# A fused two-layer graph kernel on one core: five edits at the seam between its layers and around its walk

## The chip, the core and the metric

The program runs on one core of a Trainium2 chip. Its engines are TensorE (PE; its weight loads are listed apart as PEld), VectorE (DVE), ScalarE (ACT), GpSimd (POOL) and SyncE (SP), which here issues nearly all DMAs. Each engine works through its own list of instructions, and semaphores tie them together. The metric is the time of one execution on the device in microseconds; the comparison uses the median of several runs.

## What is computed

There are 2708 nodes with 256 features, and an adjacency matrix `adj` (2708 x 2708, float32). Everything is computed in float32. Cut to what matters:

```python
# layer 0
R = adj + I;  R = R / R.sum(-1)
for n in range(2):
    A  = top_p(softmax(q(Xa) @ k(Xa).T), 0.9)   # rows renormalised
    Xf = R @ Xf                                 # the "walk"
    Xa = A @ Xa                                 # the "attention"
    Z += Xf @ U1[n].T + Xa @ U2[n].T
h = layernorm(x + Z) * ln_g + ln_b
x = layernorm(x + h)
# layer 1: graph attention, 4 heads of 64
Wh = x @ W;  e_ij = leaky_relu(s_i + s_j), masked where adj is zero (diagonal kept)
x = layernorm(x + softmax_j(e) @ Wh)
```

## The kernel before

**Tiles.** The 2708 rows are cut into 22 tiles: 16 of 128 rows and 6 of 110. The last three tiles are called late (`LATE = 3`).

**Layer 0** is `fast_layer0`. It has two steps `s`, 0 and 1. In each step the attention of tile `t` runs on TensorE in six groups of up to four source tiles (`weigh`, L274: transposes of the kept probabilities, L266, copies of them by ScalarE, L271, and matmuls, L284). Beside it runs the walk, which multiplies by the adjacency matrix; it is put together from products of mixed blocks (the "mixes", written to DRAM during step 0), seven products for each of 11 pairs of row tiles, and is the generator `walks` (L1034). The walk of step 0 starts when step 0's attention is over, and reaches into step 1; the walk of step 1 ends close to the end of step 1's attention.

**Slots.** The order of work on TensorE, VectorE, ScalarE and GpSimd is written out by hand: after each group of the attention, `slot` (L1292) advances several generators by one `yield`:

- `going`: searches for the probabilities to keep of a coming tile (`search`, L971). Its first part is `scores` (L780): logits by matmul (L791) in three pieces, each exponentiated by ScalarE (L795). The first two pieces come in the slot in which the search begins, the third one slot later. A search of tile `t + 3` begins at the fifth group of tile `t`.
- `doing`: what remains to be done for a row tile after its walk or attention: `after_walk0`, `after_attention0`, `finish`, and the early loads of layer 1's masks (`early_bar`).
- `mixing` and `stream`: the mixes, and so many matmuls of the walk (L1109) as the slot's allowance says.

`finish(t, ...)` (L1261) closes a tile in step 1. ScalarE scales the walk's rows `xw` by `rinv`, the inverse row sums (L1265). GpSimd adds up x and the terms of step 0 and 1: `ca` (x), `cb` (a stored term), `xw`, and the attention's rows `held[t]` (L1270 to L1272), and adds the bias to `ca` (L1273). For tiles that aren't late, two layer norms follow (`norms`, L186) and then `sources` (L159), which projects the row by layer 1's weights: transposes (L165), a copy (L167), a matmul (L171) and seven small readings by ScalarE (L175 to L181). The late tiles wait until the walk is over (`walked`), since their sums are written over the walk's operand `xe`, and get their norms in layer 1 (`prepared`, L1665).

**Banks.** Once the walk has begun, the logits and the projections of `sources` take turns in the same pool of two PSUM buffers (`ps_lg`, through `free_bank`, L650).

**Rows of step 0.** `after_walk0` (L1194) scales and adds on GpSimd, yields once, and stores the rows to DRAM (L1200). They are read back when the walk of step 0 ends.

**SyncE** is not among the engines whose order is fixed by hand: where each of its DMAs stands in its list is set by a planner, which places a DMA once its buffer is free and its sources are there, by its own estimates of time. The list is then executed in order.

**Layer 1** (`layer1`) goes over three groups of target tiles (8, 8 and 6); for each, over all 22 source tiles `j`. VectorE makes the weights `pt` of four heads from the targets, the source's `tj` and the mask (L1606); TensorE adds up values (L1618) and denominators (L1628), two source tiles at a time. The mask is loaded (L245) and made 0 or 1 by ScalarE (L247, L248). The targets of the first group are two tiles from the pool `ep` (three buffers, shared with the probabilities of layer 0): `share` (L208) turns the sources' terms and stores them, `spread` (L219) broadcasts them back to all partitions, two DMAs for each of the two tiles. In step 1, `share(0, ...)` stands at the start of tile 20 and `spread(0, ...)` at that of tile 21 (L1315 to L1319).

**Memory.** Pools of layer 1 take the memory that pools of layer 0 leave. Among the latter is `keep`, which holds the walk's and the attention's operands and, by L632, `rinv`:

```python
rinv = keep.tile([P, NT], F32, name="rinv")
```

Tiles of the pool `const` stay for the whole program.

Of the kernel before, what the change touches and what calls it, by code (L numbers as in the profile page):

```python
# [45 lines left out]
def kernel(  # L46
# [169 lines left out]
        nc.scalar.activation(line[:k, :m], tr[:k, 0, :m], AF.Exp, scale=1.0 - NEG_SLOPE)  # L216
        nc.sync.dma_start(shared[g], line[:k, :m])

    def spread(g, r):  # L219

        lines = shared[g].rearrange("(t h) m -> h t m", h=H)
        n = len(spans[g]) * rows[spans[g][0]]
        for k in range(2):
            for h in range(2):
                nc.sync.dma_start(
                    r[k][:, h, :n].rearrange("p (t m) -> p t m", t=len(spans[g])),
                    lines[2 * k + h].partition_broadcast(P),
                )
# [22 lines left out]
            nc.vector.tensor_tensor(own, own, ident[:k, :k], op=ALU.max)  # L251
        yield bar

    def room(pool):

        return [
            pool.tile([P, N], F32, name="e")[:, : 2 * GW].rearrange("p (h i) -> p h i", h=2)
            for _ in range(2)
        ]

    def turned(e, m, n, pool, ps, copy):
# [290 lines left out]
    def fast_layer0(ep, adjp):  # L552
# [76 lines left out]


        kT = [wk.tile([P, HN], F32, name="junk"), keep.tile([P, HN], F32, name="kT1")]
        rinv = keep.tile([P, NT], F32, name="rinv")  # L632

        BLOCKS = ("D11", "S2", "S3", "S1", "D22", "S4")
        mixed = {
# [398 lines left out]
        def walks():  # L1034
# [19 lines left out]
            def beside(s, t):  # L1054

                m = rows[t]
                if s and t >= NT - LATE:
                    ca = x_late[:, t - NT + LATE, :]
                    nc.gpsimd.memset(ca[:, 0:1], 0.0)
                else:  # L1060
                    ca = finp.tile([P, D], F32, name="ca", bufs=4)
                if not s:
                    nc.sync.dma_start(ca[:m], c1[t][:m])
                    return ca, None
                cb = finp.tile([P, D], F32, name="cb")
                nc.sync.dma_start(ca[:m], x[off[t] : off[t + 1], :])
                nc.sync.dma_start(cb[:m], c2[t][:m])
                if t in c3:
                    assert t in stored
                    held[t] = finp.tile([P, D], F32, name="cc")  # L1070
                    nc.sync.dma_start(held[t][:m], c3[t][:m])
                return ca, cb
# [6 lines left out]
            for at, (s, i, n) in enumerate(queue):  # L1079
# [17 lines left out]
                        home = dict(X=k, Y=1 - k, Z=k, W=1 - k)  # L1097
                if at % 7 == (3 if s else 0):
                    aside = {t: beside(s, t) for t in (a, b)}
                start = chain not in use  # L1100
                if start:
                    pool, label = (ps_wk, f"walk{home[chain]}") if home[chain] < 2 else (ps_at, "att")
# [91 lines left out]
        def after_walk0(t, xw, ca, _):  # L1194
            m = rows[t]
            yield
            nc.gpsimd.tensor_scalar(xw, xw, rinv[:m, t : t + 1], None, op0=ALU.mult)
            nc.gpsimd.tensor_add(xw, xw, ca[:m])
            yield
            nc.sync.dma_start(xmd[:m, t], xw)  # L1200
            rows_kept.append(t)

# [44 lines left out]
        def terms2(t, xT):  # L1247
# [10 lines left out]
            nc.scalar.copy(ba[:m, t, :], cy[:m, D : 2 * D])  # L1258
            nc.sync.dma_start(c2[t][:m], cs[:m])

        def finish(t, xw, ca, cb):  # L1261

            m = rows[t]
            yield
            nc.scalar.activation(xw, xw, AF.Copy, scale=rinv[:m, t : t + 1])  # L1265
            while t not in held or (t >= NT - LATE and not walked):
                yield
            late = t >= NT - LATE
            xt = xe[:m, t, 0:D] if late else lines[t % len(lines)][:m]
            nc.gpsimd.tensor_add(xt, ca[:m], cb[:m])  # L1270
            nc.gpsimd.tensor_add(xt, xt, xw)
            nc.gpsimd.tensor_add(xt, xt, held.pop(t)[:m])  # L1272
            nc.gpsimd.tensor_add(ca[:m], ca[:m], b_sb[:m])  # L1273
            if not late:
                yield
                yield from norms(t, xt, ca)
                yield from sources(t, rowp, free_bank, src=xt)
                nc.sync.dma_start(xd[:m, t], xt)


        going, doing, stored, owing = [], [], set(), set()
        early, walked, blending, begun, rows_kept = [], [], [], [], []
        ready, held = {}, {}
        stream, mixing = walks(), mixes()
# [2 lines left out]
        def advance(parts):  # L1287
            for g in list(parts):
                if next(g, parts) is parts:
                    parts.remove(g)  # L1290

        def slot(spend, begin=None):  # L1292

            advance(going)
            if begin and begin[1] < NT:
                going.append(search(*begin))
                next(going[-1])
            advance(doing)
            if begun:
                next(mixing, None)  # L1300
            owed[0] += spend
            while owed[0] > 0:
                owed[0] -= 1
                if next(stream, True):
                    break

        def step(s, cur, spend):
            turned_first = None
            for t in range(NT):
                m = rows[t]  # L1310
                e, rden = ready[t]
                ac = ps_at.tile([P, CHUNK], F32, name="att")
                if s == 0 and t == NT - 1:
                    list(mixing)
                if s and t == NT - 2:  # L1315
                    share(0, free_bank())
                if s and t == NT - 1:
                    ahead.extend(room(ep))
                    spread(0, ahead)  # L1319

                def between(n):
                    last = n == len(groups) - 1
                    if last:
                        xa = heldp.tile([P, D], F32, name="xa1")
                        nc.scalar.activation(xa[:m], ac[:m, :D], AF.Copy, scale=rden)  # L1325
                        if s and t in c3:
                            nc.scalar.dma_start(c3[t][:m], xa[:m])
                            stored.add(t)
                        elif s:
                            held[t] = xa  # L1330
                        else:
                            doing.append(after_attention0(t, xa))
                    if (s, t) == (0, NT - 1):
                        for name, at in (("T3", 1), ("T2", 2), ("T1", 2), ("T4", 4)):
                            if n == at:
                                for part in J_PARTS:
                                    blend(name, *part)
                        if last:
                            next(stream)
                    slot(spend[n], (s, t + 3) if n == len(groups) - 2 else None)  # L1340

                def turn_next(n):
                    u = t + n // len(groups)
                    if u == NT:
                        return None
                    return turned(ready[u][0], rows[u], n % len(groups), tpp, ps_tr, nc.scalar.copy)

                turned_first = weigh(
                    ac[:m, :D], turned_first or turn_next(0), m,
                    lambda j: cur[: rows[j], j, 0:D], turn_next, between,  # L1350
                )
                ready.pop(t)
# [478 lines left out]
```

## Time and profile before

| What | us |
|---|---|
| median of 3 runs | 1532.81 (1531.89 to 1533.17) |
| the profiled execution, its own time | 1534.79 |
| its span, from the first to the last instruction | 1532.7 |
| walk of step 0, from and to (about) | 442 to 800 |
| last matmul of the walk of step 1 | 1177.9 |
| first weights of layer 1 on VectorE | 1183.58 |
| last matmul of the attention (about) | 1188.7 |

Times within the execution are counted from its first instruction. A line of the timeline gives start, duration, engine, line, operation, what is written and read, the count of instructions merged, and in brackets how long the engine had been idle before it and what ended that. "x8" with 12.81 us is the time from the first to the last of eight. The ends of matmuls are modelled, so a busy TensorE need not be one at its peak. SPq and ACTq are the sequencers of SyncE and ScalarE: they issue DMAs.

### The profile page before, as it was taken

How to read it: one execution, taken by the hardware profiler on the slowest of the kernel's cores; microseconds unless marked ns; L12 is line 12 of the kernel's file. 1: busy time of each engine (PE TensorE's matmuls, PEld its weight loads, DVE VectorE, ACT ScalarE, POOL GpSimd, SP SyncE). 2: the span in 40 equal slices, each digit the busy share in tenths (PEclk: the TensorE clock that was granted, in tenths of full speed). 3: DMA queues.
4: the chain of work that ended last, by engine and by line, in shares of the span. 5: the costliest groups of instructions: out<-in, count | busy, mean ns of one | idle time of the engine just before them, and what ended most of it. 6: DMA issues, size and time to landing. Idle time of an engine off the chain costs nothing. (4 is left out here: it accounts for less than half of the span.)

```text
span 1532.7 us, 29967 instructions
## 1 busy us (share of the span) xinstructions
PE 1492.8 (97%) x10537; PEld 1064.6 (69%) x10537; DVE 1277.1 (83%) x3749; ACT 804.9 (53%) x1495; POOL 594.5 (39%) x959
## 2 busy tenths in 40 slices
PE   8999999999999999999999999999999999999996
PEld 4477777776778889988988888887898223433343
DVE  3699888999714978888889898989895998999996
ACT  3444444444326556655655666666653344456474
POOL 0046657566013323323454554544444310035143
PEclk9999999999999999999999999999999999999998
DMA  6288888878037755554564555555455355334331
GB/s 166 66 246 277 247 247 281 266 234 255 12 102 235 211 165 167 161 162 137 159 199 142 165 183 170 182 166 178 137 151 178 109 172 167 100 104 135 88 105 53
DMA packets 214488, 255.97 MB, mean 167 GB/s; under 512 B 42145, under 2 KB 180541, under 8 KB 214329
## 3 DMA queue, kind: packets, MB, share of 16 engines
q1 hardware_dynamic: 205622, 246.62, 53.7%
q10 hardware_dynamic: 8707, 7.35, 1.5%
q8 instruction: 85, 1.39, 0.4%
q14 instruction: 74, 0.61, 0.1%
HBM read 190.10 MB, written 62.44 MB: 165 GB/s over the span
## 5 line engine op out<-in xcount | busy, mean ns | idle before, releaser
L816 ACT ACTIVATE junk<-e,minus,rth 128x2708 bf16<-128x2708 f32 (+1 forms) x88 | 232.9, 2646 | 52.5 <-POOL rth L848 51.7
L271 ACT COPY eT<-tr 128x512 f32<-128x512 f32 (+5 forms) x264 | 141.5, 536 | 199.0 <-PE tr L266 196.5
L284 PE MATMUL att<-xm,eT 128*128 128x256 f32 (+3 forms) x968 | 230.8, 379 | 0.3 <-ACT xa L1325 0.3
L284 PE MATMUL att<-ba,eT 128*128 128x256 f32 (+3 forms) x968 | 230.9, 379 | 0.0
L1618 PE MATMUL acc<-pt,v 128*32 128x512 f32 (+3 forms) x2112 | 222.9, 543 | 2.1 <-DVE pt L1606 1.1
L1606 DVE SCALAR_TENSOR_TENSOR pt<-e,tj,blk 128x1024 f32<-128x1024 f32 (+3 forms) x176 | 186.6, 1125 | 8.3 <-ACT xw L1265 5.4
L284 PEld LDWEIGHTS att<-xm,eT 128*128 128x128 f32 (+3 forms) x968 | 169.6, 186 | 22.0 <-ACT xa L1325 0.7
L284 PEld LDWEIGHTS att<-ba,eT 128*128 128x128 f32 (+3 forms) x968 | 169.5, 186 | 22.0 <-ACT eT L271 0.8
L795 ACT ACTIVATE e<-lg 128x1024 f32<-128x1024 f32 (+1 forms) x132 | 121.0, 921 | 105.7 <-PE lg L791 102.2
L1109 PE MATMUL walk<-xe,blk 128*128 128x128 f32 (+3 forms) x1386 | 172.9, 275 | 1.2 <-ACT xw L1123 0.7
L1109 PEld LDWEIGHTS walk<-xe,blk 128*128 128x128 f32 (+1 forms) x1386 | 164.4, 187 | 11.4 <-issue 7.4
L1618 PEld LDWEIGHTS acc<-pt,v 128*32 128x32 f32 (+1 forms) x2112 | 73.4, 109 | 130.8 <-issue 76.2
L266 PE MATMUL tr<-ident,e 128*128 128x128 f32 (+3 forms) x968 | 147.5, 271 | 4.8 <-ACT eT L271 4.8
L266 PEld LDWEIGHTS tr<-ident,e 128*128 128x128 f32 (+3 forms) x968 | 111.3, 139 | 47.1 <-issue 26.7
L1109 PE MATMUL walk<-xm,blk 128*128 128x128 f32 (+3 forms) x1034 | 131.3, 277 | 5.4 <-DVE u_sb L1119 2.9
L1109 PEld LDWEIGHTS walk<-xm,blk 128*128 128x128 f32 (+3 forms) x1034 | 124.2, 188 | 14.0 <-issue 6.1
L1628 PE MATMUL acc<-pt,sb 128*32 128x512 f32 (+3 forms) x1056 | 115.7, 542 | 0.0
L1606 DVE SCALAR_TENSOR_TENSOR pt<-r,tj,blk 128x1024 f32<-128x1024 f32 (+1 forms) x88 | 109.9, 1312 | 1.3 <-issue 0.6
L247 ACT ACTIVATE blk<-blk 128x1024 f32<-128x1024 f32 (+3 forms) x66 | 63.3, 960 | 82.5 <-DMA blk<-in_adjT_dram 76.2
L896 DVE MAX8 cand<-e 128x8 f32<-128x170 f32 (+1 forms) x352 | 85.9, 320 | 21.1 <-ACT e L795 21.0
L896 DVE MAX8 cand<-scr 128x8 f32<-128x97 f32 (+1 forms) x616 | 102.8, 244 | 0.0
L914 DVE MAX8 top<-work 128x8 f32<-128x128 f32 (+3 forms) x242 | 82.3, 340 | 8.3
(283 smaller groups left out, 2410.2 us busy)
## 6 DMA issues: line engine op xcount, KB each, us to landing
blk<-in_adjT_dram SPq DMA_DIRECT2D x68, 512.0 KB
blk<-S SPq DMA_DIRECT2D x48, 512.0 KB
blk<-D SPq DMA_DIRECT2D x24, 512.0 KB
blk<-in_adjT_dram SPq DMA_DIRECT2D x26, 440.0 KB
D<-blk SPq DMA_DIRECT2D x16, 512.0 KB
S<-scr SPq DMA_DIRECT2D x16, 512.0 KB
S<-blk SPq DMA_DIRECT2D x16, 512.0 KB
xm<-S SPq DMA_DIRECT2D x16, 512.0 KB
```

Source lines behind the costliest of these rows:

```text
L247: nc.scalar.activation(bar, bar, AF.Sign)
L266: nc.tensor.transpose(tr[: rows[t], q, :m], e[:m, off[t] : off[t + 1]], ident[:m, :m])
L271: copy(eT[:k, : len(grp), :m], tr[:k, : len(grp), :m])
L284: nc.tensor.matmul(acc, eT[: rows[t], q, :m], value(t), start=(t == 0), stop=(t == NT - 1),)
L795: nc.scalar.activation(halves[:m, :, c0 : c0 + w], lg[:m, :, :w], AF.Exp, accum_out=zp[:m, n : n + 1],)
L816: nc.scalar.activation(junk[:m], e[:m], func, scale=rth, bias=minus1[:m], accum_out=acc)
L896: nc.vector.max(cand[:, n, :], src[:m, n * size : min(N, (n + 1) * size)])
L914: nc.vector.max(top[:, k : k + 8], work if k else flat)
L1109: nc.tensor.matmul(ac, blk[:k, j, :], MOVING[name](j, k, w), start=start and j == 0, stop=j == PAIRS - 1, skip_group_check=True,)
L1606: nc.vector.scalar_tensor_tensor(pt[:k, :gw], targets[g][h // 2][:k, h % 2, :gw], tj[:k, j, h : h + 1], bar, op0=ALU.max, op1=ALU.mult,)
L1618: nc.tensor.matmul(acc[h // 2][c][to : to + SIDE, :w], v[j][:k, h, o : o + SIDE], probs[n][h][:k, c0 : c0 + w], **at,)
L1628: nc.tensor.matmul(acc[2][c][h * SIDE : (h + 1) * SIDE, :w], sb[:k, j, h : h + 1].to_broadcast([k, SIDE]), probs[n][h][:k, c0 : c0 + w], **at,
```

## The change

- `rinv` moves from `keep` to `const`.
- A new generator `early_sums` is started for each late tile when its loads are issued in step 1. Three slots later GpSimd adds `ca` to `cb` and the bias to `ca`; once the attention's rows are there it adds them too (`summed`). `finish` then waits for `summed` and `walked`, and does one addition for such a tile.
- `share(0, ...)` moves from tile 20 to tile 19. The targets of the first group are allocated and broadcast one at a time, the first at tile 20, the second at tile 21.
- `after_walk0` yields three times before its store rather than once, for tiles 0 to 15; tiles 16 to 21 stay as they are.
- `slot` advances `doing` before it begins a new search rather than after it.

```diff
-    def spread(g, r):
+    def spread(g, r, these=(0, 1)):
...
-        for k in range(2):
+        for k in these:
...
-    def room(pool):
+    def room(pool, count=2):
...
-            for _ in range(2)
+            for _ in range(count)
...
-        rinv = keep.tile([P, NT], F32, name="rinv")
+        rinv = const.tile([P, NT], F32, name="rinv")
...
                 if at % 7 == (3 if s else 0):
                     aside = {t: beside(s, t) for t in (a, b)}
+                    for t in (a, b):
+                        if s and t >= NT - LATE:
+                            doing.append(early_sums(t, *aside[t]))
+                            next(doing[-1])
...
             nc.gpsimd.tensor_add(xw, xw, ca[:m])
-            yield
+            for _ in range(3 if t < NT - 6 else 1):
+                yield
             nc.sync.dma_start(xmd[:m, t], xw)
...
+        def early_sums(t, ca, cb):
+
+            m = rows[t]
+            for _ in range(3):
+                yield
+            nc.gpsimd.tensor_add(cb[:m], cb[:m], ca[:m])
+            nc.gpsimd.tensor_add(ca[:m], ca[:m], b_sb[:m])
+            while t not in held:
+                yield
+            summed[t] = held.pop(t)
+            nc.gpsimd.tensor_add(summed[t][:m], summed[t][:m], cb[:m])
...
             nc.scalar.activation(xw, xw, AF.Copy, scale=rinv[:m, t : t + 1])
-            while t not in held or (t >= NT - LATE and not walked):
+            late = t >= NT - LATE
+            if late:
+                while t not in summed or not walked:
+                    yield
+                nc.gpsimd.tensor_add(xe[:m, t, 0:D], summed[t][:m], xw)
+                return
+            while t not in held:
                 yield
-            late = t >= NT - LATE
-            xt = xe[:m, t, 0:D] if late else lines[t % len(lines)][:m]
+            xt = lines[t % len(lines)][:m]
...
             advance(going)
+            advance(doing)
             if begin and begin[1] < NT:
                 going.append(search(*begin))
                 next(going[-1])
-            advance(doing)
...
-                if s and t == NT - 2:
+                if s and t == NT - 3:
                     share(0, free_bank())
-                if s and t == NT - 1:
-                    ahead.extend(room(ep))
-                    spread(0, ahead)
+                if s and t >= NT - 2:
+                    ahead.extend(room(ep, 1))
+                    spread(0, ahead, (len(ahead) - 1,))
```

More of the change, by code (lines that the diff above doesn't have):

```diff
@@ L1273, in finish @@
             nc.gpsimd.tensor_add(ca[:m], ca[:m], b_sb[:m])
[L1274 to L1281, printed above, removed]
+            yield
+            yield from norms(t, xt, ca)
+            yield from sources(t, rowp, free_bank, src=xt)
+            nc.sync.dma_start(xd[:m, t], xt)
+        going, doing, stored, owing, summed = [], [], set(), set(), {}
         early, walked, blending, begun, rows_kept = [], [], [], [], []
```

## The prediction

> **What bounds the kernel now.** First the page's engine shares, then the busy time of the engines in seven stretches that I cut at the walk's end (1178 us) and at layer 1's three groups of targets.
>
> ```profile
> PE 1492.8 (97%) x10537; PEld 1064.6 (69%) x10537; DVE 1277.1 (83%) x3749; ACT 804.9 (53%) x1495; POOL 594.5 (39%) x959
> ...
> 441.00:850.00 409.00, 400.85 (x2891) 354.63 (x2890) 320.74 (x1225) 236.20 (x325) 141.09 (x291) 1.00 0.58 175
> 850.00:1178.00 328.00, 324.08 (x2304) 285.74 (x2303) 286.53 (x1088) 196.53 (x394) 150.40 (x292) 1.00 0.56 168
> 1178.00:1186.00 8.00, 6.71 (x36) 5.23 (x35) 2.63 (x3) 6.81 (x16) 5.35 (x7) 1.00 0.51 176
> 1186.00:1200.00 14.00, 12.85 (x94) 3.55 (x96) 13.93 (x13) 4.58 (x6) 10.69 (x7) 1.00 0.32 94
> 1200.00:1268.00 68.00, 67.42 (x581) 19.99 (x577) 67.24 (x82) 30.77 (x45) 11.43 (x6) 1.00 0.50 150
> ```
>
> Columns: stretch, length, busy PE, PE loads, VectorE, ScalarE, GpSimd, clock, DMA share, GB/s. While the walks run, TensorE binds: it idles 8 of 409 and 4 of 328 us, in pieces that can be counted. From 1186 to 1268 VectorE is full (81.2 of 82 us) and feeds TensorE. TensorE seems nearly full too, but in its timeline the value matmuls of the first pair of source tiles run from 1186.34 to 1198.35, 12.0 us, and those of later pairs in 7.1. So what delays VectorE here delays everything after. It idles 5.37 us just before; the view of tile rinv says for what, and the timelines of VectorE, GpSimd and ScalarE show the place:
>
> ```profile
>   DVE pt L1606: 5.4, 1
> ...
> 1183.58 12.81 DVE L1606 SCALAR_TENSOR_TENSOR pt<-e,tj,blk 128x1024 f32<-128x1024 f32 x8 [5.37 <-ACT xw L1265]
> ...
> 1183.69 1.76 POOL L1271 TENSOR_TENSOR xe<-xe,xw 110x256 f32<-110x256 f32 x1 [2.42 <-ACT xw L1265]
> 1185.53 1.60 POOL L1272 TENSOR_TENSOR xe<-xe,xa 110x256 f32<-110x256 f32 x1
> ...
> 1180.25 1.06 ACT L248 ACTIVATE blk<-blk 128x1024 f32<-128x1024 f32 x1
> 1181.21 0.49 ACT L1265 ACTIVATE xw<-xw,rinv 110x256 f32<-110x256 f32 x1
> ...
> 1183.02 0.52 ACT L1265 ACTIVATE xw<-xw,rinv 110x256 f32<-110x256 f32 x1
> ```
>
> The first weights need the first mask (L248, ended 1181.31), yet begin 0.04 us after the last scaling by rinv (1183.54): rinv lies in a pool of layer 0 whose memory they reuse. Then eight weights take 12.81 us; the next eight take 9.66. Seven GpSimd additions run through them until 1195.3, at 1.5 to 1.76 us each, where the same additions took 0.63 to 0.73 before 1181.
>
> In layer 0, the timelines of SyncE and TensorE around 495 us, and the logits of one begin slot:
>
> ```profile
> 491.77 0.33 SPq L1200 DMA_DIRECT2D xmd<-xw  x1
> 492.19 0.82 SPq L689 DMA_DIRECT2D blk<-S  x2
> 493.49 0.32 SPq L1200 DMA_DIRECT2D xmd<-xw  x1
> ...
> 496.89 2.69 PE L1109 MATMUL walk<-xm,blk 128*128 128x128 f32 x22 [1.75 <-DMA blk<-S]
> 499.82 0.35 PE L1109 MATMUL walk<-xe,xm 128*128 128x128 f32 x1 [0.24 <-DMA xm<-S]
> ...
> 1071.56 0.44 PE L165 MATMUL lg<-ident,u_sb 128*128 128x128 f32 x2 [0.36 <-ACT e L795]
> 1072.57 0.44 PE L165 MATMUL lg<-ident,u_sb 128*128 128x128 f32 x2 [0.56 <-ACT e L795]
> ```
>
> A store held SyncE for a GpSimd result, the block behind it came late, and TensorE idled 1.75 and 0.24 us. In four begin slots (1005, 1037, 1069, 1103 us) the projection's transposes or matmuls wait for a PSUM bank that the new logits hold: 0.36, 0.36, 0.36+0.56, 0.36, together 2.0 us.
>
> **What the Trainium skill says.** "SBUF — State Buffer", section "Who interferes with whom": a VectorE instruction with two SBUF inputs contends with a GpSimd instruction that reads SBUF. The trace agrees: 1.66 to 1.76 us per weight with GpSimd busy, 1.28 without. "Perfetto Trace Analysis", section "Identifying the Most-Contended Engine": matmul busy time doesn't tell how near TensorE is to its limit. Agreed: 12.85 of 14 us busy while starved. Same page, "Sequencer Loop": each sequencer takes instructions in order, which is why a waiting store holds the load behind it (491.77, then 492.19).
>
> **The change, part by part.**
>
> *rinv among the constants.* Nothing is computed differently. The wait for L1265 goes; next is the mask, at 1181.31. The landed first half of the targets (issued 1148.31) and TensorE's last walk matmul (1177.9) are earlier. 1183.58 - 1181.35 = **2.2 us**. If another tile of the same pools is read as late, it is nought.
>
> *Late rows' sums ahead.* Per late row four GpSimd additions after the walk become one; the others move into slots where GpSimd idles (8.25 us before 1177.75), waiting there for loads of ca and cb issued around 1168. The third row's last attention ends at 1189.2, so two of its additions (sum, final) stay, and one of the second row's: three additions of 1.6 us inside the eight weights instead of seven. A weight beside GpSimd starts 1.67 us after its predecessor, one alone 1.20. Three additions cover 4.8 us, some three weights: 3 x 0.47 = 1.4 us lost, against 12.81 - 9.66 = 3.15 now: **1.75 us**. Bounds: 3.15 if none collides; 0 if cb of the last row is loaded so late that its two early additions fall back among the weights.
>
> Both: eight weights end at 1181.35 + 9.66 + 1.4 = 1192.4 rather than 1196.39, 4.0 us earlier. The second mask ends only at 1186.81, where the fifth weight wants it at about 1186.6; so **3.8**. Does it reach the end? TensorE finishes attention at 1188.7 and, no longer starved, gains about 12.0 - 7.1 - 2.3 (attention in between) = 2.6 on the first pair, and the rest in pairs four and five, which last 12.1 and 11.35 us now against 10.3 and in which it waits for VectorE (weights ending 1229.3 and 1240.6). By 1246 the whole 3.8 is through. The 5.73 us stall of VectorE at 1274 (masks landing behind the next group's targets) hangs on loads issued at fixed places of the program, so it moves along.
>
> *Stores two slots on.* Sixteen stores, none added. At 495 us 1.99 us of idle can go. But VectorE waits for TensorE only 1.18 us there (497.49 to 498.67) and at 510.9 its addition L1129 again holds TensorE 0.76 us; what TensorE gains beyond 1.2 it waits there. **1.2 us**, bounds 0 (a planner sets SyncE's order) and 2.0. The other waits of L1200 cost nothing: TensorE has no idle for a DMA after 500 us. The xw buffer (four, so two pairs of some 21 us) is still free in time: four slots of 3.9 us plus the transfer.
>
> *Norms ahead of logits.* In those slots the projection comes first and the logits wait. By the same two banks: at 1005 one L171 (1.16 us), then ScalarE's seven small readings to about 2.7 us after the start, while the first half of the logits covers to 2.15: 0.6 lost for 0.36. At 1037 L171 and a transpose end at 1.6, and the first logits wait to 2.7: 1.1 for 0.36. At 1069 two transposes: 0.2 for 0.92. At 1103: 0 for 0.36. Sum 1.9 for 2.0: **0**, bounds -1.5 and +1.0. Other begin slots have nothing of the kind: walk matmuls follow directly.
>
> *Halves.* share moves one tile forward (0.27 us of TensorE, 0.27 of ScalarE, and its store, in tile 19's start instead of 20's), the first two broadcasts one tile, the last two stay. In the trace the first pair was issued at 1148.31 already, 35 us before use, behind nothing: **0**. Cover gone, each broadcast pair would cost its landing, which the slow rival prices.
>
> Sum: -2.2 - 1.75 + 0.2 - 1.2 + 0 = **-5.0 us**. Against the profiled execution (span 1532.7, time 1534.79, so 2.1 us around it) that is 1529.8. The three timed runs have a median of 1532.81, 2.0 below that execution; I predict 1532.8 - 5.0 = **1527.8 us**. This measurement tells about 0.2% (3.1 us) from no change.
>
> **Rivals.**
>
> *Only one of the two ends of layer 0 is won* (0.22): another release than rinv's holds the first weights until 1183, or a load pins the late additions, and the stores give 1.2. For it: the weights wait on many semaphores, and the trace tells only the last. Against: the other ones had been passed by 1178.3. Then -1.2 to -3: about 1531.
>
> *More is won* (0.13): the first mask lands at 1179.1, ten us after its issue at 1169.18, behind the second half of the targets (1168.07). With the halves apart SyncE may put the mask first; ScalarE then doesn't stand 1.34 us in front of it, nor TensorE 1.29 us at 1180.88 for the copy behind. With the logits at no cost (2.0): -5.0 - 1.3 - 1.5 = 1525.
>
> *Slower* (0.12): SyncE's order is set by a planner, and new release points for xw, ca, cb and the targets re-order its loads of walk blocks. The unit price is the 1.75 us above, each time a block comes late. Three late blocks (5.25 us) eat the 5.0, from five on (8.75) the change is slower by over 0.2%, and seven (12.25) give 1540. Against: since 500 us no block is late, with three in flight; for: SyncE waits 184 us in all for walk buffers, so its order matters. The same price holds for the second targets: from a landing at about 1187 the third weight waits as long as the whole gain.
>
> **How the numbers follow.** Forecast 0.53 (1525.5 to 1530, its own range), the rivals 0.22, 0.13 and 0.12. Range 1523.0 to 1535.0: it leaves out the lower tail of the rival at 1525 and nearly all of the slow one, some 0.17 together. Faster by over 0.2%: nearly all of 0.53, 0.13 and a small part of the 0.22: 0.68. Within: most of 0.22: 0.20. Slower: 0.12.
>
> **What would show it.** The first weight should start at about 1181.4 on the old scale (3.5 us after the walk's last matmul), released by L248; the first eight should take about 11 us with three GpSimd additions beside them; pairs four and five of layer 1 should last some 10.5 us. TensorE should not wait for a block at 495. Transposes L165 should wait for no exp, and a logit matmul should wait for L181 at 1005 and 1037. I am wrong if the first weight still starts 5 us after the walk, if seven additions still run beside it, or if TensorE waits for DMAs between 500 and 1178 us.

## The result and the profile after

The changed kernel takes 1530.65 us (median of 14 runs, 1528.07 to 1534.78) against 1533.48 us for the kernel before beside it (14 runs, 1531.85 to 1538.46). The ratio is 0.9977, 95% interval 0.9969 to 0.9986: 3.5 us faster, with an interval of 2.1 to 4.8 us (the two medians lie 2.8 us apart). The forecast was 5.0 us, a little above that interval; the measured median lies outside the forecast's own 1525.5 to 1530 us and near the 1531 of the first rival. The profiled execution took 1529.34 us, its span 1527.4 us.

First come the page's engine shares, then the busy time of the engines in the stretches that were shown for the kernel before, each moved with the walk's end (columns: stretch, length, busy PE, PE loads, VectorE, ScalarE, GpSimd, clock, DMA share, GB/s):

```profile
PE 1488.8 (97%) x10537; PEld 1066.7 (70%) x10537; DVE 1291.6 (85%) x3749; ACT 805.4 (53%) x1495; POOL 603.8 (40%) x959
...
441.00:848.00 407.00, 398.67 (x2887) 352.95 (x2887) 320.36 (x1223) 236.36 (x324) 142.64 (x290) 1.00 0.58 175
848.00:1176.20 328.20, 324.72 (x2307) 286.37 (x2306) 290.21 (x1090) 196.58 (x394) 162.29 (x300) 1.00 0.56 168
1176.20:1184.20 8.00, 5.67 (x27) 4.11 (x26) 3.83 (x4) 5.85 (x15) 1.17 (x2) 0.91 0.54 197
1184.20:1198.20 14.00, 14.00 (x107) 5.62 (x109) 13.49 (x14) 7.57 (x9) 3.82 (x3) 0.93 0.37 107
1198.20:1266.20 68.00, 67.86 (x597) 22.71 (x590) 66.17 (x82) 29.76 (x45) 11.43 (x6) 1.00 0.52 160
```

GpSimd's work has left the stretch of the first weights (10.69 us of 14 before, 3.82 now) and gone into the walk (150.40 before, 162.29 now). VectorE has become busier in the walk too (286.53 before, 290.21 now), though the change gives it nothing to do there; that comes back below. Right after the walk TensorE is busy only 5.67 of 8 us, where it was 6.71.

The seam itself, in the timelines of VectorE, then ScalarE, then GpSimd of the changed kernel:

```profile
1176.04 0.29 DVE L1133 TENSOR_TENSOR xw<-walk,u_sb 110x128 f32<-110x128 f32 x1 [4.42 <-PE walk L1113]
1180.50 5.34 DVE L1627 SCALAR_TENSOR_TENSOR pt<-e,tj,blk 128x1024 f32<-128x1024 f32 x4 [4.17 <-DMA blk<-in_adjT_dram]
1186.01 4.87 DVE L1627 SCALAR_TENSOR_TENSOR pt<-e,tj,blk 128x1024 f32<-128x1024 f32 x4 [0.16 <-ACT blk L248]
```

```profile
1178.32 1.06 ACT L247 ACTIVATE blk<-blk 128x1024 f32<-128x1024 f32 x1 [2.38 <-DMA blk<-in_adjT_dram]
1179.41 1.06 ACT L248 ACTIVATE blk<-blk 128x1024 f32<-128x1024 f32 x1
```

```profile
1182.79 0.78 POOL L1287 TENSOR_TENSOR xe<-xa,xw 110x256 f32<-110x256 f32 x1 [6.20 <-ACT xw L1282]
1189.88 1.60 POOL L1276 TENSOR_TENSOR xa<-xa,cb 110x256 f32<-110x256 f32 x1 [6.31 <-ACT xa L1346]
...
1191.56 0.74 POOL L1287 TENSOR_TENSOR xe<-xa,xw 110x256 f32<-110x256 f32 x1
```

The first weight begins 0.03 us after the first mask is done (1179.41 + 1.06 = 1180.47), no longer after the last scaling by `rinv`. The eight weights take 1190.88 - 1180.50 = 10.38 us with a wait of 0.16 inside, where they took 12.81. But the wait in front of them fell only from 5.37 to 4.17 us: ScalarE idles 2.38 us for the mask's transfer, and so gets to the mask 2.28 us after VectorE's last addition of the walk began (1.24 us before). TensorE waits for ScalarE's copy behind the mask:

```profile
1177.94 1.05 PE L171 MATMUL lg<-wx,xT 128*110 128x264 f32 x4
1181.33 0.59 PE L266 MATMUL tr<-ident,e 110*110 110x110 f32 x4 [2.33 <-ACT eT L271]
```

That wait was 1.29 us before. In layer 0, the timelines of SyncE and TensorE near 495 and 510 us, and the view of the logits' line between 1000 and 1110 us:

```profile
491.34 0.33 SPq L1205 DMA_DIRECT2D xmd<-xw  x1
491.76 0.83 SPq L689 DMA_DIRECT2D blk<-S  x2
...
496.41 2.69 PE L1113 MATMUL walk<-xm,blk 128*128 128x128 f32 x22 [1.74 <-DMA blk<-S]
...
510.84 1.38 PE L1113 MATMUL walk<-xm,blk 128*128 128x128 f32 x10 [1.30 <-DVE xw L1133]
```

```profile
  ACT cs L181: 1.2, 2
  ACT xT L167: 0.2, 1
```

The store still stands at the head of SyncE at 491.34, and TensorE still waits 1.74 us for the block behind it. The logits now wait for the projection's readings, as worked out, but for less: 0.18, 1.01 and 0.25 us in TensorE's timeline (1005.44, 1036.40 and 1068.61), 1.44 in place of 2.0.

### The profile page after: what moved, and what is told of

It reads as the page before. It is cut to its first block, busy times and chain, and to the rows that moved or that the text cites. A ratio compares the mean times of both kernels' runs of the same rounds, so it can differ in the third digit from the quotient of the medians.

```text
span 1527.4 us, 29965 instructions
## 1 busy us (share of the span) xinstructions
PE 1488.8 (97%) x10537; PEld 1066.7 (70%) x10537; DVE 1291.6 (85%) x3749; ACT 805.4 (53%) x1495; POOL 603.8 (40%) x959
## 5 line engine op out<-in xcount | busy, mean ns | idle before, releaser
L1639 PE MATMUL acc<-pt,v 128*32 128x512 f32 (+3 forms) x2112 | 216.0, 543 | 0.6
L247 ACT ACTIVATE blk<-blk 128x1024 f32<-128x1024 f32 (+3 forms) x66 | 63.3, 962 | 78.2 <-DMA blk<-in_adjT_dram 71.3
L802 POOL TENSOR_TENSOR fact<-zp 128x1 f32<-128x1 f32 (+1 forms) x44 | 37.7, 856 | 146.8 <-ACT e L795 146.8
```

The source lines that it names most:

```text
L247: nc.scalar.activation(bar, bar, AF.Sign)
L802: nc.gpsimd.tensor_add(z, zp[:m, 0:1], zp[:m, 1:2])
L1639: nc.tensor.matmul(acc[h // 2][c][to : to + SIDE, :w], v[j][:k, h, o : o + SIDE], probs[n][h][:k, c0 : c0 + w], **at,)
```

## The experiments

For the seam (the passage from the walk's end into layer 1) one number of each trace doesn't contain the time lost or won before it: from the start of VectorE's last addition of the walk to the end of the eighth weight. It is 0.29 us for the addition, the wait, and the weights with the waits among them. Before: 0.29 + 5.37 + 12.81 = 18.47 us. Changed: 0.29 + 4.17 + 10.38 = 14.84 us. The table gives it for each kernel, with the lead by which SyncE issued the first mask ahead of that addition. Each is one execution; the same mask took 9.6 to 10.8 us from issue to ScalarE's start on it in the kernels with unchanged queues, so some tenths are chance. "The same" and "the same less" refer to the kernel with the second half and `v` from ScalarE.

| Kernel | Mask's lead | Wait | Eight weights | Seam | Ratio to before (95%) |
|---|---|---|---|---|---|
| before | 8.74 | 5.37 | 12.81 | 18.47 | 1 |
| `rinv` alone | 8.71 | 2.89 | 12.33 | 15.51 | 0.9970 (0.9960 to 0.9980) |
| early sums alone | 7.93 | 6.36 | 11.20 | 17.85 | 0.9993 (0.9985 to 1.0000) |
| both | 7.86 | 3.65 | 11.33 | 15.28 | 0.9980 (0.9971 to 0.9988) |
| norms ahead alone | 8.75 | 6.17 | 12.83 | 19.29 | 0.9992 (0.9984 to 1.0000) |
| stores alone | 8.73 | 5.67 | 12.81 | 18.78 | 1.0005 (0.9996 to 1.0015) |
| halves alone | 8.75 | 5.50 | 12.81 | 18.60 | 1.0006 (0.9997 to 1.0014) |
| the change | 7.91 | 4.17 | 10.38 | 14.84 | 0.9977 (0.9969 to 0.9986) |
| second half from ScalarE | 7.63 | 1.69 | 11.67 | 13.65 | 0.9974 (0.9963 to 0.9986) |
| and `v` from ScalarE, first set | 9.02 | 1.69 | 11.67 | 13.65 | 0.9963 (0.9949 to 0.9976) |
| the same, second set | 9.03 | 1.69 | 11.67 | 13.65 | 0.9964 (0.9952 to 0.9977) |
| the same less early sums | 9.84 | 1.69 | 13.29 | 15.27 | 0.9978 (0.9969 to 0.9986) |
| the same less `rinv` | 9.02 | 4.26 | 11.19 | 15.74 | 0.9972 (0.9960 to 0.9984) |
| the same, stores from ScalarE | 9.01 | 1.69 | 11.76 | 13.74 | 0.9967 (0.9955 to 0.9979) |

Whether a shorter seam gets through to TensorE can be read from the end of the fifth pair of source tiles, counted from the same addition. TensorE's timeline of the kernel before, then of the changed one:

```profile
1242.00 4.02 PE L1628 MATMUL acc<-pt,sb 110*32 110x512 f32 x30
```

```profile
1237.39 4.02 PE L1649 MATMUL acc<-pt,sb 110*32 110x512 f32 x30
```

Before: 1246.02 - 1177.92 = 68.10 us. In every kernel of the table but one the gain there equals that of the seam to 0.02 us. The one is the change: 1241.41 - 1176.04 = 65.37, a gain of 2.7 us where its seam gained 3.6. In that execution TensorE ran at half clock from 1182.8 to 1186.2, early in the weights, and was busy for all of the 14 us from 1184.2: there TensorE, and no longer VectorE, set the pace. So the 14.84 overstates what the change won.

### One part alone: rinv, early sums, both

```diff
-        rinv = keep.tile([P, NT], F32, name="rinv")
+        rinv = const.tile([P, NT], F32, name="rinv")
```

> Kernel before with rinv among the constants and nothing else; the order of instructions on every engine is that of before. Theory (rinv's wait is real and is 2.2 us): the first weights are released by the first mask (L248) rather than by L1265, 0.04 us after it; VectorE's idle before them falls from 5.37 to about 3.2 us; eight weights still take about 12.8 us, since seven GpSimd additions still run beside them or ahead of them (about 12.4 if the second mask isn't late). Whole kernel 1.5 to 2.2 us faster. Rival (another release stands behind rinv's): idle still above 5 us and time as before. Rival (the gain is swallowed on the way): idle 3.2 us, but the ends of the later pairs of source tiles and the whole time as before.

Measured: 1530.36 us (9 runs; before 1533.89). The order of the instructions is that of the kernel before on every engine; only a wait is gone. VectorE's timeline:

```profile
1181.84 12.33 DVE L1606 SCALAR_TENSOR_TENSOR pt<-e,tj,blk 128x1024 f32<-128x1024 f32 x8 [2.89 <-DMA blk<-in_adjT_dram]
```

The wait fell by 5.37 - 2.89 = 2.48 us. Some 0.2 us of this is the mask's landing, since ScalarE idled 1.10 us in front of it and 1.34 before. This edit alone gives as much as the whole change.

The early sums alone are the change's `early_sums`, its call in the walk and the shortened `finish`, with `rinv` where it was:

```diff
+                    for t in (a, b):
+                        if s and t >= NT - LATE:
+                            doing.append(early_sums(t, *aside[t]))
+                            next(doing[-1])
```

> Kernel before with the late rows' early sums alone. Theory: the first weights still wait for L1265 (idle about 5.4 us), but of seven additions beside the first eight weights three stay or fewer, and the eight take 10.4 to 11.1 us rather than 12.8; whole kernel 1.7 to 2.4 us faster. Rival (the additions fall back among the weights because their loads come late): 12 us or more for the eight, and no gain.

Measured: 1533.08 us (22 runs). The weights are shorter by 1.6 us, but the wait ahead of them grew by 1.0; what is left can hardly be told from nothing. Both edits together:

> rinv and early sums together, nothing else. Theory (the seam makes the whole gain of the change): idle before the first weights 3.2 to 4.2 us, eight weights in 10.4 to 11.1 us, whole kernel 3 to 4 us faster, that is as much as the full change within its interval (ratio 0.9977). Rival (the stores, the halves or the slot order carry a good part): at most 2 us faster, and the full change's remainder is in them.

Measured: 1530.84 us (19 runs), no faster than `rinv` alone.

```profile
1181.01 5.35 DVE L1626 SCALAR_TENSOR_TENSOR pt<-e,tj,blk 128x1024 f32<-128x1024 f32 x4 [3.65 <-DMA blk<-in_adjT_dram]
1186.51 5.83 DVE L1626 SCALAR_TENSOR_TENSOR pt<-e,tj,blk 128x1024 f32<-128x1024 f32 x4 [0.15 <-ACT blk L248]
```

Again the weights gain (12.33 to 11.33 us with the wait) and the wait loses (2.89 to 3.65). So the early sums have a cost, and the table shows where: in all three kernels that have them and leave the queues alone SyncE issues the first mask 7.86 to 7.93 us ahead of the walk's last addition, in the five without them 8.71 to 8.75 us; with the queues changed the same edit takes the lead from 9.84 to 9.03. Something makes SyncE 0.8 us late. Here are VectorE's timeline some 35 us earlier and the links that are named below, with `rinv` alone:

```profile
1139.09 0.16 DVE L878 TENSOR_TENSOR hi<-hi,huge 110x1 f32<-110x1 f32 x1
...
1142.36 0.16 DVE L884 TENSOR_TENSOR rest<-low,fact 110x1 f32<-110x1 f32 x1
1142.56 0.16 DVE L885 TENSOR_TENSOR rest<-rest,tau 110x1 f32<-110x1 f32 x1
...
1162.39 0.41 DVE L141 TENSOR_SCALAR u_sb<-u_sb,ln_mv,ln_rs 110x256 f32<-110x256 f32 x1
...
1167.20 0.30 SPq L1066 DMA_DIRECT2D x_late<-in_x_dram  x1
```

The same, and then GpSimd's timeline, with both edits:

```profile
1137.24 0.71 DVE L878 TENSOR_TENSOR hi<-hi,huge 110x1 f32<-110x1 f32 x1
1137.98 3.04 DVE L881 SCALAR_TENSOR_TENSOR scr<-e,hi 110x2708 f32<-110x2708 f32 x1
...
1141.06 0.56 DVE L884 TENSOR_TENSOR rest<-low,fact 110x1 f32<-110x1 f32 x1
1141.66 0.66 DVE L885 TENSOR_TENSOR rest<-rest,tau 110x1 f32<-110x1 f32 x1
...
1161.59 0.40 DVE L141 TENSOR_SCALAR u_sb<-u_sb,ln_mv,ln_rs 110x256 f32<-110x256 f32 x1
...
1166.40 0.30 SPq L1066 DMA_DIRECT2D x_late<-in_x_dram  x1
```

```profile
1137.20 0.73 POOL L1271 TENSOR_TENSOR x_late<-x_late,b_sb 110x256 f32<-110x256 f32 x1
1138.75 2.86 POOL L1275 TENSOR_TENSOR xa<-xa,cb 110x256 f32<-110x256 f32 x1 [0.82 <-DMA blk<-S]
1141.57 0.72 POOL L1291 TENSOR_TENSOR u_sb<-ca,cb 110x256 f32<-110x256 f32 x1
```

Operations on one number per partition take 0.56 to 0.71 us instead of 0.16, each beside a GpSimd addition: 0.55 + 0.40 + 0.50 = 1.45 us on VectorE, of which smaller meetings of the old order elsewhere give a part back. In the other direction one addition takes 2.86 us, until VectorE's long pass over `e` has ended. "SBUF — State Buffer", section "Who interferes with whom", of the Trainium skill states that a VectorE tensor_tensor with both inputs in SBUF contends with GpSimd's reads; the trace agrees, and gives the size. VectorE then comes 0.8 us later to the norm L141 of the row ahead (15.47 us ahead of the walk's last addition instead of 16.27); GpSimd's norm (L190, L191) follows, it stands in front of the clearing of `x_late` (L1059), the load of `x_late` (L1066) waits for that (10.66 us ahead instead of 11.46), and on SyncE the second half of the targets and the first mask stand behind it. That TensorE's walk isn't late with them is what turns 0.8 us of VectorE into 0.8 us of wait. This chain is read from the traces; no run put the early additions in another place.

### One part alone: norms ahead, stores, halves

```diff
             advance(going)
+            advance(doing)
             if begin and begin[1] < NT:
                 going.append(search(*begin))
                 next(going[-1])
-            advance(doing)
```

> Kernel before with doing advanced ahead of a new search in each slot, nothing else. Theory: the waits of projections for exps at 1005, 1037, 1069 and 1105 us (2.0 us in all) go, and waits of logits for the seven readings L181 come, about 1.0 us at 1037 and 0.2 each at 1005 and 1069: net 0.5 us faster in these four slots, 0 to 0.5 us in the whole time, not to be told from no change. Rival (a real gain): over 1.5 us. Rival (the new wait costs more than the old): slower by 0.5 us or more.

Measured: 1533.32 us (14 runs), 0.9992. Its logits wait for the projection 1.4 us in all, and the 2.0 us of before are gone, as in the change. The 0.6 us stand in the trace; the time of the whole can hardly tell them from nothing.

```diff
-            yield
+            for _ in range(3 if t < NT - 6 else 1):
+                yield
             nc.sync.dma_start(xmd[:m, t], xw)
```

> The kernel before with the row stores alone two slots on. Theory of the prediction: the store leaves SyncE's way at 491 us, the block behind it lands in time, TensorE's idle of 1.75 and 0.24 us at 495 to 500 us goes and about 1.2 us of it reach the end (ratio about 0.9992). Rival, from the trace of the changed kernel (SyncE held by a store at 491.34 and TensorE idle 1.74 us at 494.67 there): SyncE's order around that point stays as it was, TensorE still idles 1.7 us there and the whole is within 0.5 us of before.

Measured: 1534.58 us (13 runs; before 1533.52), 1.0005. TensorE's timeline:

```profile
496.49 2.69 PE L1109 MATMUL walk<-xm,blk 128*128 128x128 f32 x22 [2.23 <-DMA blk<-S]
```

The wait at 495 us stays, as the rival had it that was taken from the changed kernel's trace.

The halves alone (with `spread` and `room` as in the change):

```diff
...
-                if s and t == NT - 2:
+                if s and t == NT - 3:
                     share(0, free_bank())
-                if s and t == NT - 1:
-                    ahead.extend(room(ep))
-                    spread(0, ahead)
+                if s and t >= NT - 2:
+                    ahead.extend(room(ep, 1))
+                    spread(0, ahead, (len(ahead) - 1,))
```

> The kernel before with the first targets in two halves alone. Theory of the prediction: 0. The share and the first half are issued some 20 us earlier, the second half still stands in front of the first mask, and the first weights are held by the scaling with rinv at about 1183.5 us anyhow: the gap before them stays 5.4 us and the whole within 0.5 us. Rival: the earlier pair takes the place of a block or of a cb load, a TensorE gap of over 0.3 us appears between 1100 and 1178 us or a late addition moves, and it costs 0.5 to 2 us.

Measured: 1534.52 us (21 runs), 1.0006: nothing, as forecast. SyncE's order differs only in the place of the share's store and of the first half; the second half stays right in front of the first mask.

### Taking the targets away from in front of the mask

If the mask's landing holds the seam of the changed kernel, the mask must gain when less stands ahead of it. The changed kernel, with the second half of the targets issued from ScalarE's queue in the first group of the last tile:

```diff
-    def spread(g, r, these=(0, 1)):
+    def spread(g, r, these=(0, 1), queue=nc.sync):
...
-                nc.sync.dma_start(
+                queue.dma_start(
...
-                    spread(0, ahead, (len(ahead) - 1,))
+                if s and t == NT - 2:
+                    spread(0, ahead, (0,))
...
+                    if s and t == NT - 1 and n == 0:
+                        spread(0, ahead, (1,), nc.scalar)
```

> The changed kernel with the second half of the first targets issued by ScalarE's queue in the first group of the last target tile, so that it no longer stands ahead of the first mask on SyncE; three small loads of v now stand there instead. Theory (the landing of the first mask, 1178.3 us, bounds the first weights and TensorE's last turns): the mask lands 0.5 to 3 us earlier after the walk's end, the gap before the first weights falls from 4.17 to 1.5 to 3.5 us, TensorE's idle of 2.33 us at 1179 shrinks or goes, the whole is 0.5 to 2.5 us faster than the changed kernel, about 1528 to 1530 us. Rival (the landing is limited by the bytes in flight, or the later weights and the second mask bind): the gap stays near 4 us or is paid back in the first eight weights, and the whole is within 0.5 us of the changed kernel.

Measured: 1529.34 us (7 runs), 0.9974. VectorE's timeline:

```profile
1177.46 5.35 DVE L1630 SCALAR_TENSOR_TENSOR pt<-e,tj,blk 128x1024 f32<-128x1024 f32 x4 [1.69 <-ACT blk L248]
1183.30 5.83 DVE L1630 SCALAR_TENSOR_TENSOR pt<-e,tj,blk 128x1024 f32<-128x1024 f32 x4 [0.49 <-ACT blk L248]
```

The wait falls from 4.17 to 1.69 us although the mask was issued no earlier against the walk (lead 7.63). The issues of the mask by SyncE and of the broadcasts by ScalarE:

```profile
1167.85 0.38 SPq L245 DMA_DIRECT2D blk<-in_adjT_dram  x1
1168.95 1.25 ACTq L225 DMA_DIRECT2D e<-shared  x2
```

What counts is not only when SyncE comes to the mask but what was issued ahead of it. In the change two broadcasts of 512 KB each stood before a mask of 512 KB; here they come 1.1 us after it. "DMA: Bandwidth & Descriptors", section "Queues, rings and completion order", of the Trainium skill says that each DMA engine takes the descriptors of one ring in order and goes round between the rings. The run is in keeping with that but doesn't single it out, because with the other queue came another order; no run kept the broadcasts on SyncE and put them behind the mask. The issue of the mask itself took 2.49 us on SyncE behind the broadcasts and 0.38 us here.

The next run has nothing of layer 1 ahead of the mask on SyncE, since the first three loads of `v` come from ScalarE's queue too:

```diff
-                    (nc.sync if n < DEEP else nc.scalar).dma_start(
+                    nc.scalar.dma_start(
```

> As the run before it (second half of the first targets from ScalarE's queue), and the first three loads of v from ScalarE's queue too, so that on SyncE nothing of layer 1 stands ahead of the first mask. Theory (landing of the first mask bounds the start of layer 1): the mask is issued about 1 us and lands 2 to 4 us earlier than in the changed kernel, the gap before the first weights is 1.5 to 2.5 us, TensorE doesn't idle 2.3 us at 1179, the whole is 1 to 3 us faster than the changed kernel, about 1528 us. Rival: a load of v waits at the head of ScalarE's order and holds the turned copies behind it (TensorE idle over 0.5 us at 1168 to 1174 by a copy of ScalarE): no gain or a loss of up to 2 us.

Measured: 1526.83 us (5 runs; before 1533.52), 0.9963. As the base of the last set it ran again:

> The kernel of the last run of the set before (changed kernel, second half of the first targets and the first three v loads from ScalarE's queue), once more, as the base for the three that follow. Theory: the same gap of about 1.7 us before the first weights and about 0.35% faster than before (ratio 0.9955 to 0.9975). Rival: its few runs were a lucky set, and it stands with the changed kernel at 0.998.

Measured: 1528.36 us (7 runs; before 1533.96), 0.9964. SyncE's, ScalarE's and TensorE's side of this second one, its timelines and one stretch of its busy time:

```profile
1166.50 0.36 SPq L245 DMA_DIRECT2D blk<-in_adjT_dram  x1
```

```profile
1175.09 0.34 ACT L167 COPY xT<-lg 128x220 f32<-128x220 f32 x1 [1.34 <-PE lg L165]
1175.32 1.06 ACT L247 ACTIVATE blk<-blk 128x1024 f32<-128x1024 f32 x1
```

```profile
1176.20:1184.20 8.00, 8.00 (x44) 5.32 (x43) 6.20 (x5) 7.73 (x18) 1.64 (x1) 1.00 0.61 179
```

ScalarE starts on the mask right behind its copy, with no idle time; TensorE is busy 8.00 of the 8 us after the walk, where it was 5.67. Twice this kernel came out some 0.36% faster than before, about 5.5 us, against 0.23% for the change. Its interval (0.9952 to 0.9977) still overlaps that of the change (0.9969 to 0.9986); that it is the better of the two rests on both sets agreeing and on the fifth pair, which in each trace ends 2.1 us earlier against the walk's last addition (63.3 us against 65.37).

### What the two seam edits are worth once the mask is early

That kernel without the early sums, and that kernel with `rinv` in its old pool, each otherwise unchanged:

> As the base, with the late rows' early sums undone alone: seven GpSimd additions beside the first eight weights again. Theory A (the early sums were worth nothing in the changed kernel only because they pushed the first mask 0.8 us later and the mask bound; with the mask out of the way their saving shows): the first eight weights and the wait inside them take 12.8 us instead of 5.35 + 0.49 + 5.83 = 11.7, the gap before them stays 1.5 to 1.9 us, and the whole is 0.8 to 1.5 us slower than the base. Theory B (what the weights gain is waited for later by VectorE or TensorE in any case): weights longer, the whole within 0.5 us of the base.

Measured: 1530.11 us (16 runs), 0.9978, against 0.9964 for the base.

```profile
1177.61 13.29 DVE L1610 SCALAR_TENSOR_TENSOR pt<-e,tj,blk 128x1024 f32<-128x1024 f32 x8 [1.69 <-ACT blk L248]
```

The same wait, and the weights 13.29 us instead of 11.67: the early sums are worth 1.6 us in the seam here, and about as much in the whole (1.75 us between the medians, with intervals that overlap). Beside `rinv`, with the queues as they were, they were worth 0.2 in the seam (15.51 to 15.28).

> As the base, with rinv back in its old pool alone. Theory (rinv's release holds the first weights whenever the mask doesn't): the first weights start when the second scaling with rinv ends, about 2.5 us later than in the base, the wait for the second mask (0.49 us) goes, the whole is about 2.0 us slower than the base. Rival: the scaling moves ahead together with the mask on ScalarE and the loss is under 0.7 us.

Measured: 1529.75 us (7 runs), 0.9972. VectorE's and ScalarE's timelines:

```profile
1180.55 11.19 DVE L1630 SCALAR_TENSOR_TENSOR pt<-e,tj,blk 128x1024 f32<-128x1024 f32 x8 [4.26 <-DMA blk<-in_adjT_dram]
...
1180.00 0.52 ACT L1282 ACTIVATE xw<-xw,rinv 110x256 f32<-110x256 f32 x1
```

The name of the releaser misleads here: the DMA had landed long before (ScalarE began on the mask at 1175.79). The start, 1180.55, is the end of the second scaling by `rinv` (1180.00 + 0.52) plus 0.03. 15.74 - 13.65 = 2.1 us, the expected size in the trace; the medians show 1.4, with intervals that overlap.

### The store taken off SyncE

```diff
-            nc.sync.dma_start(xmd[:m, t], xw)
+            nc.scalar.dma_start(xmd[:m, t], xw)
```

> As the base, with the row stores issued from ScalarE's queue instead of SyncE's. Theory of the prediction's third term (a store holds SyncE at 491 us, and TensorE idles about 2 us at 495 to 500 us for the blocks behind it; 1.2 us of it reach the end): the idle at 495 to 500 us falls below 0.5 us, the whole is about 1.2 us faster than the base. Rival 1: the idle at 495 is paid back as waits for VectorE at 510 and ScalarE at 514: idle at 495 gone, those two grow by as much, the whole within 0.4 us. Rival 2: stores waiting at the head of ScalarE hold its exps, and the whole is 1 us or more slower.

Measured: 1529.06 us (6 runs), 0.9967: nothing gained. SyncE's timeline, the view of its waits from 484 to 497 us, and TensorE's timeline:

```profile
490.87 0.33 SPq L1063 DMA_DIRECT2D ca<-c  x1
491.29 0.81 SPq L689 DMA_DIRECT2D blk<-S  x2
```

```profile
SPq L1063 <- POOL xw L1202: 5.4, 1, 5.4
```

```profile
495.84 2.69 PE L1113 MATMUL walk<-xm,blk 128*128 128x128 f32 x22 [1.65 <-DVE wants L947]
```

No store stands on SyncE, yet it waits the same 5.4 us for the same addition of GpSimd. The next load of `ca` wants the buffer that this addition reads, and the planner has put it where the store stood; in the base it stood behind these blocks, at 494.83. (TensorE's wait is put down to an instruction of VectorE here; the blocks were issued at 491.29 as late as before, and nothing else of the walk changed.) Neither the theory nor its two rivals came true: the idle time neither went nor moved, because another DMA that waits for the same addition took the store's place.

## Why the prediction was right in direction, and where its sum was off

**rinv among the constants, -2.2.** Right in mechanism and size: alone it took 2.48 us off the wait, of which 0.2 belong to the mask's landing, and 2.1 with the mask out of the way. The measured 0.30% of that run (4.6 us, interval 3.1 to 6.1) lies above both and above the 2.96 us of its seam. The more has no place in its trace; a part of it may be a mix of clocks (see the last section). Between runs with the same recorded mean clock the gap is 3.0 us at 0.995 (3 runs against 21) and 3.1 at 0.996 (5 against 12).

**Early sums, -1.75.** Right as the price of the additions (1.6 us with the mask early; the eight weights of the change take 10.38 us, where "about 11" was forecast). The failed step is that the other additions "move into slots where GpSimd idles" at no cost. GpSimd idled there, VectorE did not: the additions lengthened its small operations, and by the chain above the first mask was issued 0.8 us later. The step "next is the mask, at 1181.31" took the mask to stay where it was while the walk's end stayed too.

**Both, -3.8.** The seam shortened by 18.47 - 14.84 = 3.6 us, near the forecast but not by the forecast's route, and in part by luck. The wait is longer than worked out (the first weight came 4.5 us after TensorE's last walk matmul at 1176.0, not 3.5), the weights are shorter. Some 1 us of that (10.38 against 11.33 with both seam edits) is there because in the half clock the last attention and its additions came late and fell behind the weights. But TensorE paid for that: by the end of the fifth pair 2.7 us are left. Without such a stretch at the seam the pair of edits has 15.28, and its 3.2 us reach the end of the fifth pair whole. That pair still takes 11.35 us and not "some 10.5"; only the fourth got shorter (10.60 from 12.10).

**Stores two slots on, -1.2.** This is the term that failed outright: 0, in the change, alone, and with the store taken off the queue. The store did hold SyncE, for 5.3 us in the view of its waits. The step that failed is "At 495 us 1.99 us of idle can go". The planner left that store in front of the blocks in SyncE's list although it stood two slots later in the program, as the lower bound of 0 had allowed for; and with the store gone it put there a load that waits for the same addition.

**Norms ahead of logits, 0.** The waits appeared where they were named (L181 at 1005 and 1037 us, none of L165 for an exp), 1.44 us in place of the 1.9 worked out, so that 0.6 us were won where nought was put.

**Halves, 0.** Right.

By the traces the change is worth 2.7 + 0.6 + 0 = 3.3 us, or 3.8 with the 3.2 us of both seam edits at full clock; both lie within the measured 2.1 to 4.8. The forecast had 3.8 + 0 + 1.2. The two profiles lie 5.3 us apart: 3.4 us after the walk's last addition (1532.7 - 1177.92 against 1527.4 - 1176.04) and 1.9 ahead of it. Of the 1.9, 0.6 are the logits' waits. The rest is no more than what a stretch of half clock at 801.5 us costs, which the profile of before has and the one after has not (last section).

**The rivals.** "Only one of the two ends of layer 0 is won" came true for the stores' end, and for a third reason beside the two given; the measured 1530.65 is near its 1531, though `rinv`'s release did hold the first weights and no load pinned the late additions. "More is won" had the right mechanism with its price: it put 1.3 us on the mask standing behind the second half of the targets, and the seam gained 1.2 us against the change, 1.6 against both seam edits, when that was taken away. What it had wrong is that the halves would do this by themselves; the planner kept them in front of the mask. Nothing of the slow rival showed: no block came late after 500 us.

## What to carry to other kernels

When a wait is removed, look at what lands next and what was issued ahead of it in its own queue: here 1 MB ahead on the same queue cost about as much as the second edit could win. Issuing that 1 MB from another queue, and so behind the mask, won what the forecast had promised. Work that is moved to an idle engine is not free if it slows an engine that is busy at that time: ask for the neighbour's chain too. And before an instruction that waits at the head of a queue is moved, ask who sets the order of that queue, and what would stand there in its place.

## What the runs showed of the hardware

Short VectorE operations suffer most from a GpSimd addition beside them: a `tensor_tensor` on 110 x 1 numbers went from 0.16 to 0.56 to 0.71 us, a weight of 128 x 1024 from 1.28 to about 1.7; and a GpSimd addition of 110 x 256 from 0.73 to 2.86 us beside a VectorE pass of 3.04 us.

TensorE's clock is at half in the last 8 to 12 us of every profile. Apart from that, seven of the fourteen profiles hold one stretch of 3.4 us at half clock: near 802 us in four (before, `rinv` alone, both, stores from ScalarE), near 1182 us in two (early sums alone, the change) and at 497 us in one (less early sums). The busy time of the engines around it, in the kernel before and in the changed one:

```profile
801.50:804.90 3.40, 2.85 (x13) 2.85 (x14) 3.07 (x15) 1.76 (x3) 0.00 (x0) 0.50 0.35 133
```

```profile
1182.80:1186.20 3.40, 3.40 (x10) 2.42 (x9) 3.24 (x4) 3.40 (x6) 0.77 (x1) 0.50 0.15 39
```

Each of the seven begins after TensorE had been short of work: of the 3.4 us before it, TensorE was busy 1.1 to 1.4. The two near 1182 us follow the two longest waits for ScalarE's copy behind the late mask (2.28 and 2.33 us), so the stretch in the change is perhaps not chance alone. But lack of work doesn't suffice: from 798.3 to 801.7 us the changed kernel's TensorE was busy only 0.66 us, and its clock stayed full. What decides stays open.

The four kernels with the stretch near 802 us come to the walk's last addition at 1177.06 to 1178.66 us, the other ten at 1174.83 to 1176.16. On average that is 2 us, which is of the size of the single edits here. The runs show the same: among the 111 runs of the kernel before that stand beside the experiments, the 18 with a recorded mean clock of 0.997 took 1532.4 us on average and the 5 with 0.993 took 1538.5. So two profiles are compared stage by stage and not by their spans, and runs best at the same mean clock.
